# Three microseconds more on every transfer, in the account that orders a three-layer kernel

## The chip, the cores and the metric

The kernel runs on one core of one Trainium2 chip. The metric is the device time of one execution in microseconds (us); the median of several executions is compared. The engines are called PE (matrix products), DVE (vector), ACT (scalar, activations), POOL (general) and SP (which here only issues transfers).

## The reference

The input is a batch of 8 images with 256 channels and 32 x 32 positions. Two layers follow each other:

```python
# layer 0: convolution and attention, on group-normalised x
q  = einsum(x, q_w);  k_map, v_map = einsum(x, kv_w)
ks, vs = layernorm(pooled(k_map)), layernorm(pooled(v_map))   # 4 pooling levels, each + 3x3 depthwise conv: 1426 keys
att = softmax(q @ k * SCALE) @ v                              # 8 heads of 32 channels, 1024 queries
x = x + proj(att @ w_attn)                                    # w_attn: a small matrix per head, from a global token
# layer 1: t = tokens of x, (8, 1024, 256)
t = t + softmax(q @ k * SCALE) @ v                            # one head, of layernorm(t)
t = t + sum_e gate_e * Wo_e(relu(bn(W2_e relu(bn(W1_e layernorm(t))))))   # 8 experts, all of them used
```

The gates are a softmax over the 8 experts of the mean over the batch of the normalised tokens. Everything is float32.

## The kernel before

The kernel has two stages in one program: `attention` (layer 0, and layer 1's attention woven into it) and `experts`.

The backbone of `attention` is a loop over 352 score steps. For each image there are two groups of four heads and two halves of the queries, which makes 32 units; a unit goes through 11 chunks of 128 keys, and a twelfth chunk of 25 keys is handled for four units of an image at once. A step multiplies queries with keys into the score buffer `sc` (four banks of PSUM, one buffer), ACT takes the exponential into a tile `pt` (128 x 2048 floats, 1 MB, six buffers), and one step later PE multiplies `pt` with the values into `pv`. For the sums of the softmax the second `pt` of each two steps is added onto the first by a transfer on POOL's queue (`add`, with `accum_op=ALU.add`): this is the group pt<-pt in the profile. The thread `sums` takes the pairs on from there. In the first four units PE sums each pair directly; from the fifth on DVE adds each pair to the unit's first (two additions of 128 x 1024 for a pair), and PE sums only the result. A pair's buffer is given back (`f.drop`) once that use has been put into the queue.

Everything else is background work, written as Python generators (threads) with a rank: normalising and pooling the next image (`prepare`, which starts with statistics of the freshly loaded image `xi`), convolution taps on DVE (`taps`), keys and values by tokens, the projection of layer 0, and the whole of layer 1 (`layer1`, which loads tokens `t` from memory, and `outputs`). Three more threads read loaded tiles: `weights1` at the start, `experts_ahead` late in the attention stage, and `gates` in the expert stage, which adds seven loaded images `feat` to a sum.

The order of the instructions on each engine is decided while the program is built, by the class `Flow`. It keeps an account: for each engine a clock `now`, for each tile when it is `ready`, who wrote it (`writer`, which is "DMA" for transfers) and when it was last `read`. `note` advances the account with each instruction, by costs from `cost`; `transfer` gives a transfer 2.2 us plus its share of the queues. A thread yields what it needs next: an engine, the tiles that it will read, and possibly a PSUM buffer. Between the pieces of a score step the loop calls `step`, which asks of each thread in order of rank whether it is `runnable`, and lets the first one put its next instructions into the queues. For PE a thread is runnable when its tiles are ready `MARGIN` (1.5 us) ahead of the time at which the score buffer comes free; for another engine, in these lines:

```python
now = self.now[engine]
return now <= pe + AHEAD[engine] if at <= now + 0.3 else at <= pe + NEAR[engine]
```

Here `at` is the latest ready time of the tiles, and `pe` PE's clock. For DVE, AHEAD is 4.0 and NEAR is 1.5. When the program has to wait for something definite (a free `pt`, the next image's keys), it calls `finish`, which picks by `start` in place of `runnable`. On the chip each engine works through its queue in this order and waits at an instruction whose inputs are not there yet.

In `experts` the main loop over tokens and experts is written out by hand; only `gates` and what remains of layer 1 go through `step`. While the gates are not there, units of the first two expert layers are worked ahead and stored. All instructions that go through `Flow` carry line 677 in the profile, so the groups there are told apart by the names of their tiles.

Of the kernel before, what the change touches and what calls it, by code (L numbers as in the profile page):

```python
# [33 lines left out]
CAP = (1.5, 1.5)  # L34
NEVER = 1e9
MARGIN = 1.5
AHEAD = {"DVE": 4.0, "ACT": 2.0, "POOL": 1.0, "SP": 10.0}
NEAR = {"DVE": 1.5, "ACT": 2.0, "POOL": 1.0, "SP": 10.0}
OWN = {"pt", "p1"}
# [624 lines left out]
class Flow:  # L664
# [216 lines left out]
    def spawn(self, gen, rank):  # L881
# [6 lines left out]
            self.threads.insert(at, thread)  # L888
        return thread

    def runnable(self, need, rank=0):
        engine, tiles, tag = need
        if engine is None:
            return tiles()
        at = max([self.ready.get(n, 0.0) for t in tiles for n in self.keys(t)], default=0.0)
        pe = self.now["PE"]
        if engine == "PE":

            until = max(pe, self.free("sc") - 0.5)
            slot = self.free(tag) if tag is not None else 0.0  # L900
            return (
                not self.closed
                and (self.credit[rank >= FILLER] > 0 or pe < until - 0.5)
                and at + MARGIN <= until
                and slot <= until
            )

        now = self.now[engine]
        return now <= pe + AHEAD[engine] if at <= now + 0.3 else at <= pe + NEAR[engine]

# [1981 lines left out]
```

## Time and profile before

| | us |
|---|---|
| median of 3 executions | 3219.64 |
| lowest, highest | 3211.74, 3234.84 |
| the profiled execution, its own time | 3221.01 |
| span of its instructions in the profile | 3219.2 |
| attention stage, up to the last additions of pairs | about 1850 |

The profile is of one execution. It tells each engine's busy time, which instruction it sat idle in front of, and what released it ("<-DMA pt<-pt" is the landing of a pair's transfer). The granted clock of PE was 0.986 of full speed over the span.

### The profile page before, as it was taken

How to read it: one execution, taken by the hardware profiler on the slowest of the kernel's cores; microseconds unless marked ns; L12 is line 12 of the kernel's file. 1: busy time of each engine (PE TensorE's matmuls, PEld its weight loads, DVE VectorE, ACT ScalarE, POOL GpSimd, SP SyncE). 2: the span in 40 equal slices, each digit the busy share in tenths (PEclk: the TensorE clock that was granted, in tenths of full speed). 3: DMA queues.
4: the chain of work that ended last, by engine and by line, in shares of the span. 5: the costliest groups of instructions: out<-in, count | busy, mean ns of one | idle time of the engine just before them, and what ended most of it. 6: DMA issues, size and time to landing. Idle time of an engine off the chain costs nothing.

```text
span 3219.2 us, 55913 instructions
## 1 busy us (share of the span) xinstructions
PE 3063.1 (95%) x22518; PEld 1782.2 (55%) x22518; DVE 2271.2 (71%) x3812; ACT 1624.0 (50%) x2164; POOL 1191.9 (37%) x1321
## 2 busy tenths in 40 slices
PE   7889889989999999989999999999999999999998
PEld 3232224334434433433433357776888888888887
DVE  6865786796887877866544444445887888877776
ACT  3756666567566656666655432334333333334443
POOL 3423242322331422321121120003855555567776
PEclk9899999999999999999999999999999999999999
DMA  1466756666676566566776752214444344320000
GB/s 54 87 150 151 167 117 127 155 131 130 136 169 132 118 150 137 119 152 132 167 164 124 173 212 76 86 72 156 149 146 153 139 161 161 138 78 21 20 14 21
DMA packets 123436, 397.92 MB, mean 124 GB/s; under 512 B 14928, under 2 KB 41080, under 8 KB 99712
## 3 DMA queue, kind: packets, MB, share of 16 engines
q0 software_dynamic: 28608, 181.68, 29.1%
q1 hardware_dynamic: 91056, 210.57, 19.1%
q8 instruction: 180, 2.95, 0.4%
q10 hardware_dynamic: 3504, 1.99, 0.2%
q14 instruction: 88, 0.72, 0.1%
HBM read 129.77 MB, written 97.03 MB: 70 GB/s over the span
## 4 chain that ended last, share of the span: by engine, by line
PE 45%; DVE 3%; issue 1%; POOL 1%; ACT 1%; DMA 1%; DVEq 0%; ACTq 0%; POOLq 0%
PE bank L677 21%; PE y L677 10%; PE sm L677 9%; PE sc L677 2%; PE pv L677 2%; PE sx L677 1%; DVE h L677 1%; DVE u L677 1%; DVE c L677 1%; ACT pt L677 0%; POOL t L677 0%; ACT h L677 0%; DMA pt<-pt 0%; POOL tm L677 0%; DVE t L677 0%
## 5 line engine op out<-in xcount | busy, mean ns | idle before, releaser
L677 ACT ACTIVATE pt<-sc 128x2048 f32<-128x2048 f32 (+1 forms) x352 | 660.6, 1877 | 344.5 <-PE sc L677 290.8
L677 DVE TENSOR_TENSOR pt<-pt,pt 128x1024 f32<-128x1024 f32 x280 | 341.5, 1265 | 237.4 <-DMA pt<-pt 216.0
L677 PE MATMUL sc<-q,kn 32*128 32x512 f32 (+2 forms) x3072 | 423.6, 656 | 72.1 <-ACT pt L677 68.3
L677 PE MATMUL pv<-pt,vt 128*32 128x512 f32 (+1 forms) x2816 | 384.2, 618 | 0.0
L677 POOL TENSOR_TENSOR rstd<-rstd,mhalf 128x4 f32<-128x4 f32 (+2 forms) x88 | 107.3, 1219 | 718.3 <-DVE rstd L677 640.6
L677 ACT ACTIVATE h<-h,bnvec 128x512 f32<-128x512 f32 x432 | 326.6, 805 | 66.5 <-DVE h L677 59.0
L677 ACT ACTIVATE p1c<-bank 128x256 f32<-128x256 f32 x216 | 82.7, 383 | 541.8 <-PE bank L677 524.6
L677 DVE SCALAR_TENSOR_TENSOR acc<-map,vec,acc 128x961 f32<-128x961 f32 (+1 forms) x240 | 310.2, 1295 | 25.8 <-ACT acc L677 20.0
L677 POOL DMA_DIRECT2D pt<-pt x160 | 148.8, 932 | 408.4 <-ACT pt L677 311.8
L677 DVE TENSOR_TENSOR h<-p1c,bank 128x512 f32<-128x512 f32 x216 | 147.3, 682 | 194.6 <-PE bank L677 189.3
L677 PEld LDWEIGHTS sc<-q,kn 32*128 32x128 f32 (+2 forms) x3072 | 114.5, 180 | 251.9 <-ACT pt L677 145.7
L677 DVE TENSOR_TENSOR h<-u,bank 128x256 f32<-128x256 f32 (+1 forms) x432 | 220.0, 550 | 7.4
L677 POOL TENSOR_TENSOR tm<-h,tm 128x256 f32<-128x256 f32 x190 | 218.6, 1151 | 14.9
L677 DVE SCALAR_TENSOR_TENSOR sacc<-small,vec,sacc 128x480 f32<-128x480 f32 (+8 forms) x384 | 201.7, 532 | 13.3 <-ACT sacc L677 3.3
L677 PEld LDWEIGHTS pv<-pt,vt 128*32 128x32 f32 (+1 forms) x2816 | 56.0, 108 | 276.9 <-issue 263.1
L677 PE MATMUL sm<-p,v 128*32 128x256 f32 (+1 forms) x2448 | 201.9, 380 | 4.1 <-DVE turn L677 4.1
L677 DVE TENSOR_TENSOR h<-h,gate 128x1024 f32<-128x1024 f32 x128 | 196.3, 1534 | 0.5 <-ACT h L677 0.5
L677 POOL TENSOR_TENSOR tm<-h 128x512 f32<-128x512 f32 x95 | 123.5, 1300 | 179.6 <-ACT h L677 176.3
L677 PE MATMUL y<-t,s3e 128*128 128x256 f32 x768 | 187.0, 379 | 2.2 <-POOL t L677 2.2
L677 PE MATMUL sm<-y,t 128*32 128x256 f32 (+1 forms) x1896 | 185.1, 379 | 1.2 <-DVE res L677 1.2
L677 PE MATMUL bank<-t,s1e 128*128 128x256 f32 x726 | 176.5, 379 | 0.0
L677 POOL TENSOR_TENSOR t<-h 128x512 f32<-128x512 f32 x98 | 126.7, 1293 | 133.8 <-DVE h L677 90.2
(373 smaller groups left out, 5573.1 us busy)
## 6 DMA issues: line engine op xcount, KB each, us to landing
pt<-pt POOLq DMA_DIRECT2D x160, 1024.0 KB, 7.6
h<-h SPq DMA_DIRECT2D x175, 512.0 KB
xi<-in_x_dram SPq DMA_DIRECT2D x16, 512.0 KB
t<-t SPq DMA_DIRECT2D x8, 1024.0 KB
res<-t SPq DMA_DIRECT2D x32, 256.0 KB
t<-res SPq DMA_DIRECT2D x32, 256.0 KB
hn<-res SPq DMA_DIRECT2D x32, 256.0 KB
hn<-hn SPq DMA_DIRECT2D x16, 512.0 KB
```

The lines of the kernel that those rows point to most:

```text
L677: ins = fn(*args, **kwargs)
```

## The change

A constant `LATE` of 3.0 is added, and `runnable` takes the ready time of each tile through a new method `landed`, which adds `LATE` if the tile's last writer was a transfer.

```diff
 MARGIN = 1.5
+LATE = 3.0
 AHEAD = {"DVE": 4.0, "ACT": 2.0, "POOL": 1.0, "SP": 10.0}
...
+    def landed(self, name):
+
+        return self.ready.get(name, 0.0) + LATE * (self.writer.get(name) == "DMA")
+
     def runnable(self, need, rank=0):
         engine, tiles, tag = need
         if engine is None:
             return tiles()
-        at = max([self.ready.get(n, 0.0) for t in tiles for n in self.keys(t)], default=0.0)
+        at = max([self.landed(n) for t in tiles for n in self.keys(t)], default=0.0)
         pe = self.now["PE"]
```

The account's clocks and ready times themselves, `note`, `start` and `finish` stay as they are. Weights that are loaded outside `Flow`, on ACT's queue at the start, have no writer in the account and are not affected.

## Prediction

> **What bounds the kernel now.** I read the totals first, then the stretches of the span, then what TensorE (PE) and VectorE (DVE) waited for, and last a few single waits in order of time.
>
> ```profile
> span 3219.2 us, 55913 instructions
> PE 3063.1 (95%) x22518; PEld 1782.2 (55%) x22518; DVE 2271.2 (71%) x3812; ACT 1624.0 (50%) x2164; POOL 1191.9 (37%) x1321
> ```
>
> PE is busy for 95% of the span, so all its idle time is 3219.2 - 3063.1 = 156.1 us. [...] I use it only for gaps: an order of instructions takes no matmul away, it can only open or close them. In stretches (columns: busy time of PE, its weight loads, DVE, ACT, POOL, then clock and DMA):
>
> ```profile
> 160.00:480.00 320.00, 279.36 (x2404) 95.53 (x2400) 221.46 (x396) 204.45 (x243) 98.85 (x120) 0.95 0.66 147
> 480.00:800.00 320.00, 304.42 (x3020) 125.44 (x3012) 243.90 (x429) 203.89 (x248) 86.07 (x104) 0.98 0.63 134
> 800.00:1120.00 320.00, 307.14 (x3058) 125.43 (x3062) 259.83 (x472) 200.20 (x240) 98.77 (x123) 0.99 0.65 141
> 1120.00:1440.00 320.00, 300.38 (x3056) 120.95 (x3052) 243.21 (x420) 195.72 (x231) 83.05 (x103) 0.99 0.64 140
> 1440.00:1760.00 320.00, 313.70 (x3448) 120.36 (x3440) 178.76 (x335) 192.84 (x207) 62.03 (x70) 0.99 0.69 146
> ...
> 1920.00:2240.00 320.00, 320.00 (x1282) 235.26 (x1281) 151.34 (x309) 114.95 (x191) 33.01 (x46) 1.00 0.28 99
> ```
>
> The attention stage ends near 1850. PE's gaps in the first five rows are 40.6, 15.6, 12.9, 19.6 and 6.3, together 95.0 us. From 1920 to 2240 there is none. So whatever the order account changes has to show up in those 95 us (3% of the span).
>
> Then the waits that a late transfer causes, DVE first, PE below:
>
> ```profile
> DVE pt L677 <- DMA pt<-pt: 216.0, 67, 12.1
> ...
> PE sc L677 <- ACT pt L677: 68.3, 71, 3.4
> PE sx L677 <- DMA pt<-pt: 10.1, 2, 8.5
> PE sm L677 <- DVE st L677: 5.2, 1, 5.2
> PE sm L677 <- DMA t<-t: 1.0, 1, 1.0
> ```
>
> DVE stood 216.0 us in 67 waits (3.2 us each) in front of an addition whose second operand, a pair of exponentials summed by a POOL transfer, had not landed. PE's own largest wait is another one: the next scores wait for ACT to read the one score buffer out. One piece of DVE's time shows that the 216 us are not all lost:
>
> ```profile
> 1212.70 0.16 DVE L677 SCALAR_TENSOR_TENSOR tshift<-tmean,rstd 128x4 f32<-128x4 f32 x1
> 1224.91 2.75 DVE L677 TENSOR_TENSOR pt<-pt,pt 128x1024 f32<-128x1024 f32 x2 [12.06 <-DMA pt<-pt]
> ...
> 1223.42 0.77 ACT L677 ACTIVATE acc<-sm,vec,mid 128x512 f32<-128x512 f32 x1
> ```
>
> This is the longest of the 67. Behind the additions stand convolution taps on an accumulator that ACT finished at 1224.19, so with the addition placed later DVE would have gained 0.7 of these 12.06 us. In the second longest (9.43 us, ending at 772.94) the accumulator was done at 771.05: 1.9 us. Long waits are mostly an empty queue, not a blocked one.
>
> Two places do reach PE:
>
> ```profile
> 209.74 1.94 PE L677 MATMUL sx<-pt,con 128*32 128x512 f32 x8 [8.52 <-DMA pt<-pt]
> ...
> 390.01 1.29 DVE L677 BATCH_NORM_STATS2 st<-xi 128x6 f32<-128x512 f32 x2 [5.16 <-DMA xi<-in_x_dram]
> ...
> 395.94 0.59 PE L677 MATMUL sm<-mv,con 128*128 128x2 f32 x2 [5.23 <-DVE st L677]
> ```
>
> [...] 7.6 us median to landing, 3.8 to 15.5. [...]
>
> **The change part by part.** It removes and adds no instruction, no transfer and no semaphore. It changes when a waiting thread counts as ready: if one of its tiles was last written by a transfer, three microseconds of the account's time are added. Only the test `runnable` sees them; `start`, used when the program must drain, does not, nor does the account's own clock. For a pair the account has 1.0 for the issue and 2.2 + 1048.6 KB x 0.0036 = 5.97 for the transfer, 6.97 in all, 0.6 under the trace's median; with the three it is 9.97, which covers all but the slow tail.
>
> Affected are: 140 pair additions on DVE (280 instructions), the PE sums of the first four units (24 tests), two statistics reads of the image per batch, the eight loads of layer 1's tokens, seven gate additions, and single weight loads. Not affected: everything in the expert loop after the gates, which is written out by hand, so the 980 us after 2240 keep their order except for which units were staged.
>
> *Direct waits of PE.* Placed three later, 8.5 becomes 5.5, the other PE wait for pairs (1.6) goes, 1.0 goes, 5.2 becomes 2.2: 3.0 + 1.6 + 1.0 + 3.0 = 8.6 us gained, if other PE work stands ready. Bounds: 0 (no filler) to 15.3 (waits 8.5 + 1.6 + 5.2 all gone).
>
> *DVE.* The ceiling is 67 waits x 3 us = 201 us. The two waits above gave back 2.6 of 21.5, so I take between a tenth and a half of 201, 20 to 100 us of DVE. PE gains only where it waits for DVE: from 160 to 1850 that is 4.1 (turn), 3.8 (res), 2.1 (t), 1.6 (s) and 0.9 (xl), 12.5 us without the 5.2 counted. I take a third, 4 us; bounds 0 to 12.5, and more only if earlier taps give PE fillers that it lacks (rival one).
>
> *Buffers held longer.* A pair is dropped after its second addition is queued, so it is held up to 3 us longer; there are six buffers, and a step of scores comes about every 1760/352 = 5 us. So 0.6 of the 140 pairs, 84, are held over one more step. Today ACT waits 17.5 us (8 times) for a pair's transfer before writing a buffer and about 6.5 us (3 times) for DVE, 2.2 us each. Behind that exponential on ACT stand copies of projections and convolution maps, and PE's next scores wait for it. I let one in ten of the 84 wait: 8 x 2.2 = 18 us on ACT, half of it covered by fillers on PE: 9 us lost. Bounds: 0 to 46 (half of the 84 waiting).
>
> *Layer 1's loads* are used three later eight times; 0 to 24 us, covered by other fillers; I take 2. *The gates* come after 1887.9, their last load is issued at 2174.3, and PE has no gap there to widen: 0; uncovered it would be 3. *The drain at the end of attention* goes by `start`: 0. POOL's and SP's queues get no instruction moved past them on purpose; their issues follow the threads by the same few us.
>
> Sum: -8.6 - 4 + 9 + 2 = -1.6 us against the profiled execution's 3221.01 (span 3219.2 and 1.8 around it), 3219.4. That execution stands 1.4 over the median 3219.64, so the forecast in terms of the median is 3218.
>
> **Rivals.** *One: DVE was the pacemaker.* If half of the 201 us comes back as earlier taps, the next batch's key and value work is there sooner and fills PE. For: DVE is busy 76 to 81% from 480 to 1440 and waiting much of the rest. Against: its longest waits had nothing behind them, and PE's waits for it are small. Price: 40% of the 95 us of gaps, 38: 3182.
>
> *Two, slower: the six buffers run short.* Mechanism as above, in the attention stage at the start of each exponential: half of the 84 held pairs make ACT wait 2.2 us, half of that is bare on PE: 46, less 4 that DVE still gives: 3262. It decides once ACT's waits for buffers pass some 60 us (24 today). For: those waits exist already and feed PE's largest wait. Against: 341 of 352 steps find a buffer free today.
>
> *Three: nothing reaches PE.* The account orders the same work slightly otherwise and every gap stays within a few us: 3220.
>
> **How the numbers follow.** Forecast 0.45, rival three 0.08, rival one 0.22, rival two 0.25. The forecast's own range is 3192 (both gains at their bounds, 15.3 and 12.5, nothing lost) to 3240 (nothing gained, the 18 us of ACT bare on PE, and 2). An order of thousands of instructions can move either way by more than its parts, so the range for 8 in 10 reaches to both rivals' values: 3182 to 3262. Over 1% (32 us) is about what a measurement of this kernel can tell from no change; the forecast and rival three lie within it (0.53), rival one beyond below (0.22), rival two beyond above (0.25).
>
> **What would show it.** Right: DVE's wait for pairs falls from 216 to below 170 but not to 50; PE's wait of 8.5 and of 5.2 shrink to 3 to 6; ACT's waits for buffers grow to 30 to 50; PE's gaps from 160 to 1760 stay at 80 to 110 us; 1920 to 2240 stays full. Rival one: PE's gaps fall below 65. Rival two: ACT's waits for buffers pass 60 and PE's wait of the scores for ACT passes 100. The forecast is wrong in kind if PE's busy time itself moves by over 15 us, or if the end of attention (1850) moves by over 30.

## The result, and the profile after

| | before | after |
|---|---|---|
| median, us | 3220.52 | 3178.8 (3174.91 to 3181.38) |
| ratio | | 0.9875, interval 0.985 to 0.9899 |
| span of the profiled execution, us | 3219.2 | 3176.1 |

The median of before is that of its runs beside after. The changed kernel is 1.25% faster, 42 us by these medians. The forecast was no change (3218), with 3182 as the lower end of its range. All `Flow` instructions now carry line 678.

The totals of after, at the head of its profile page:

```profile
span 3176.1 us, 56426 instructions
PE 3052.5 (96%) x22778; PEld 1794.2 (56%) x22778; DVE 2284.5 (72%) x3823; ACT 1627.8 (51%) x2175; POOL 1287.8 (41%) x1387
```

The span is 43.1 us shorter. PE's idle time went from 156.1 to 3176.1 - 3052.5 = 123.6 us, 32.5 less; its busy time fell by 10.6 us although the same result is computed. The instructions are not quite the same ones (56426 in the profile, in place of 55913), since the order also decides how products are cut up and where the function `warm` puts fillers. These are products of a constant tile with itself, issued where the account sees PE idle for 1.8 us or more. In the trace they are 40 matmuls (2.5 us) in before, 108 (9.2 us) in after. The stretches of after, with the columns as in the prediction:

```profile
160.00:480.00 320.00, 290.05 (x2670) 103.89 (x2666) 226.35 (x399) 210.50 (x256) 105.47 (x122) 0.98 0.67 147
480.00:800.00 320.00, 307.96 (x3127) 125.78 (x3120) 240.55 (x434) 202.84 (x245) 88.66 (x104) 0.99 0.65 139
800.00:1120.00 320.00, 308.61 (x3280) 124.29 (x3280) 268.21 (x494) 196.72 (x231) 97.82 (x120) 0.99 0.66 143
1120.00:1440.00 320.00, 307.91 (x3018) 123.65 (x3020) 252.88 (x425) 216.09 (x269) 100.44 (x115) 1.00 0.65 140
1440.00:1760.00 320.00, 315.05 (x3452) 126.46 (x3448) 172.75 (x329) 185.76 (x189) 61.30 (x68) 1.00 0.70 149
1920.00:2240.00 320.00, 317.02 (x1293) 240.84 (x1292) 192.71 (x309) 114.97 (x189) 120.42 (x156) 0.99 0.42 145
```

The gaps of the first five rows are 30.0, 12.0, 11.4, 12.1 and 5.0, 70.4 in all against 95.0. Each stretch gave some, but in 5.1 of the 24.6 us PE only runs more fillers. The clock column rose in four of the five rows, by 0.03 in the first and 0.01 in the others. This can be where busy time went: in before a product pv<-pt,vt of 128x512 took 614 ns in the median outside the stretches at half rate (see the last section), and 1061 ns inside them. The last row is new: it is no longer quite full (3.0 us of gaps).

The waits of after (us in total, times, longest):

```profile
DVE pt L678 <- DMA pt<-pt: 111.1, 34, 13.6
...
PE sc L678 <- ACT pt L678: 48.2, 63, 3.0
...
PE sm L678 <- DVE mv L678: 15.8, 2, 10.3
...
ACT pt L678 <- DMA pt<-pt: 12.2, 7, 3.3
...
PE sx L678 <- DMA pt<-pt: 3.5, 1, 3.5
```

DVE's wait for pairs halved, from 216.0 to 111.1. Yet all of DVE's waits from 160 to 1850 together fell only from 465 to 450: those for PE went from 109 to 178 and those for ACT from 79 to 107. What fell for PE is mostly not a wait for DVE or for a transfer: the scores' wait for ACT lost 20.1 us, the direct wait for a pair 6.6. PE's waits for DVE, all together, did not fall: from 160 to 1850 they are 17.9 us in before and 23.1 in after, while those for ACT went from 66.3 to 46.3. So the halved wait of DVE is not itself the gain.

The attention stage's last addition of a pair starts at 1830 in place of 1847, 17 us earlier. The other 26 us come later, where less of layer 1 is left to do, since more of it was done inside the attention stage. The transfers that write its tokens out (count: shortest, median and longest time of the issuing instruction in ns; then the first and the last issue in us), before and after:

```profile
L677 SPq DMA_DIRECT2D hn<-res x32: 512/528/1377, 574.0 to 2171.2; - x32
```
```profile
L678 SPq DMA_DIRECT2D hn<-res x32: 512/527/1638, 537.9 to 2063.3; - x32
```

Layer 1's last tokens leave 108 us earlier, so the gates come earlier and fewer expert units must be stored and fetched again. The page counts these transfers:

```profile
h<-h SPq DMA_DIRECT2D x175, 512.0 KB
```
```profile
h<-h SPq DMA_DIRECT2D x111, 512.0 KB
```

That is 64 transfers, a store and a fetch for 32 units.

### The profile page after: what moved, and what is told of

Read it like the earlier page. It is cut to its first block, busy times and chain, and to the rows that moved or that the text cites. A ratio compares the mean times of both kernels' runs of the same rounds, so it can differ in the third digit from the quotient of the medians.

```text
span 3176.1 us, 56426 instructions
## 1 busy us (share of the span) xinstructions
PE 3052.5 (96%) x22778; PEld 1794.2 (56%) x22778; DVE 2284.5 (72%) x3823; ACT 1627.8 (51%) x2175; POOL 1287.8 (41%) x1387
## 4 chain that ended last, share of the span: by engine, by line
PE 70%; DVE 8%; issue 3%; ACT 3%; DMA 3%; POOL 2%; SPq 0%; DVEq 0%; POOLq 0%; ACTq 0%
PE bank L678 21%; PE sm L678 16%; PE y L678 10%; PE sc L678 8%; PE sx L678 7%; PE pv L678 7%; DVE acc L678 2%; ACT pt L678 2%; DMA pt<-pt 2%; DVE pt L678 1%; DVE h L678 1%; DVE u L678 1%; DVE c L678 1%; DMA xi<-in_x_dram 1%; ACT h L678 0%
## 5 line engine op out<-in xcount | busy, mean ns | idle before, releaser
L678 PE MATMUL sc<-q,kn 32*128 32x512 f32 (+2 forms) x3072 | 417.9, 649 | 49.4 <-ACT pt L678 48.2
L678 DVE TENSOR_TENSOR pt<-pt,pt 128x1024 f32<-128x1024 f32 x280 | 340.6, 1261 | 113.9 <-DMA pt<-pt 111.1
L678 ACT ACTIVATE h<-h,bnvec 128x512 f32<-128x512 f32 x454 | 343.4, 805 | 65.8 <-DVE h L678 55.6
L678 DVE TENSOR_TENSOR h<-p1c,bank 128x512 f32<-128x512 f32 x227 | 154.7, 682 | 201.6 <-PE bank L678 198.5
L678 POOL TENSOR_TENSOR tm<-h,tm 128x256 f32<-128x256 f32 x212 | 242.8, 1145 | 16.6
L678 DVE TENSOR_TENSOR h<-u,bank 128x256 f32<-128x256 f32 x454 | 231.3, 550 | 7.8
L678 POOL TENSOR_TENSOR tm<-h 128x512 f32<-128x512 f32 x106 | 140.1, 1321 | 200.1 <-ACT h L678 198.0
L678 DVE SCALAR_TENSOR_TENSOR sacc<-small,vec,sacc 128x480 f32<-128x480 f32 (+8 forms) x384 | 194.8, 515 | 14.9 <-ACT sacc L678 4.7
L678 POOL TENSOR_TENSOR t<-h,t 128x256 f32<-128x256 f32 x218 | 173.8, 797 | 17.1
L678 POOL TENSOR_TENSOR t<-h 128x512 f32<-128x512 f32 x109 | 141.4, 1297 | 94.8 <-DVE h L678 74.1
L678 DVE TENSOR_TENSOR u<-h,bank 128x512 f32<-128x512 f32 x227 | 156.1, 688 | 25.1 <-PE bank L678 0.8
```

The source lines that it names most:

```text
L678: ins = fn(*args, **kwargs)
```

## The experiments

Three ideas run through the expectations. First, DVE's wait is itself the cost: take it away and DVE's time comes back. Second, chance: any small change gives another order of 56,000 instructions, and orders differ. Third, formed after the first results (theory C where a letter is used): DVE time that the account did not plan. If the account believed that a pair lands at the moment at which DVE reaches its addition, and it lands later, all that stands behind it on DVE, and then on ACT and PE, comes later than the order was made for. Time that DVE idles because the account planned it would cost nothing of the kind.

For the third idea each instruction's start in the account is set beside its start on the chip. Two numbers follow. The *unplanned wait* is the sum, over the first addition of each pair, of DVE's idle time in the trace beyond what the account had there. The *lag* is a DVE instruction's start in the trace less its start in the account. With the account's own end of PE's work (us; the lag near the times at the head):

```
              median  DVE wait  unplanned  account's  lag at
                      for pairs   wait      PE end    330   800  1300  1800
before        3220.5   216.0      94.2      3146.8    20.2  42.2  48.2  46.5
after         3178.8   111.1      47.3      3137.9    14.3  22.5  23.2  16.8
pairs_only    3169.4   117.2      49.3      3153.2    12.5   4.0   3.6  -6.8
all_but_pairs 3222.9   265.1     124.9      3142.3                      55.3
margin_1_4    3226.2   225.9     110.7      3147.2                      59.9
half_adds     3194.9   265.9     105.9      3120.0                      47.7
pairs_dve     3194.7   143.4      57.1      3146.6                      21.2
pairs_6       3193.6    63.0      33.0      3151.7                       7.2
pairs_m2      3285.1   289.7     148.0      3175.2                      75.5
next_pair     3231.9   129.4      76.3      3156.2                      39.3
unplanned     3257.0   177.7      76.9+97   3146.8    22.0  53.5  73.6  79.6
planned       3225.6   175.8      82.2      3150.8                      60.6
account_pool  3196.4   168.1      45.6      3170.1                      -3.7
pairs_4       3182.2    91.7      37.5      3151.9                       1.7
all_but_image 3196.3   122.2      58.1      3154.4                      19.9
pairs_pe      3221.6   254.7     112.5      3159.7                      34.6
pairs_margin  3185.5   112.1      42.9      3151.5                       7.6
```

The median is nearly the account's end plus the lag at 1800 plus a constant: over these 17 kernels the constant is 27 us with a standard deviation of 5.5. This is close to a matter of definition: it tells which of two terms a change moved, and not why. Before's lag grows to 48 and stays; pairs_only's goes back to nothing.

### Which tiles carry the gain

**pairs_only**: three microseconds for the pairs alone.

```diff
-        return self.ready.get(name, 0.0) + LATE * (self.writer.get(name) == "DMA")
+        return self.ready.get(name, 0.0) + LATE * (self.writer.get(name) == "DMA" and name.startswith("pt"))
```

> LATE of 3 us for the pairs of exponentials alone (tiles pt last written by a transfer), not for any other loaded tile. If DVE standing in front of pairs was what cost (rival one): nearly the whole gain, 3180 to 3190, DVE's wait for pairs near 110 us, PE's gaps from 160 to 1760 near 75 us. If the gain came from the image statistics, layer 1's loads or the gates: 3210 to 3225, with DVE's wait for pairs still falling to about 110. If any change of order gives a scatter of 30 to 40 us: anything from 3180 to 3250, with no relation to DVE's wait.

Measured: 3169.38, ratio 0.9845 (0.9828 to 0.9861). The pairs carry all of it. Its row for the attention stage, to set beside before's 1504.99 us of busy PE in the same window:

```profile
160.00:1760.00 1600.00, 1533.77 (x15480) 612.15 (x15474) 1166.84 (x2084) 1014.78 (x1189) 438.70 (x528) 1.00 0.67 145
```

PE's gaps are 1600 - 1533.77 = 66.2 us against 95.0; 14 of these 29 us are fillers (16.8 us against 2.5). The account of this order ends 6 us later than before's; the lag fell by 53. The gain is in the lag alone.

**all_but_pairs**: the same line with `and not name.startswith("pt")`.

> LATE of 3 us for every loaded tile except the pairs of exponentials. If the pairs carry the gain: 3210 to 3225, DVE's wait for pairs stays near 216 us; a few us may come from the PE wait of 5.2 behind the image statistics. If the other loads carry it: 3180 to 3190. If order scatter: anything from 3180 to 3250.

Measured: 3222.93, ratio 1.0015 (1.0003 to 1.0027). The image, layer 1's tokens, the gates' loads and the single weights bring nothing together.

**all_but_image**: with `and not name.startswith("xi")`, so that of all loads only the image is left out.

> The changed kernel, but without LATE for the freshly loaded image xi (LATE for pairs, tokens, gates and weights stays). In the changed kernel PE waits 15.8 us for the image's statistics (two waits, the longer 10.3), with pairs alone 9.1. If placing those statistics later is what costs the 10 us between pairs alone and the whole change: 3167 to 3174. If it is scatter of the order: 3174 to 3190.

Measured: 3196.29, ratio 0.9938 (0.9918 to 0.9958). This is 17.5 us over after. Both ranges expected lie below it. Either the image is worth that much beside the pairs, which pairs_only (9 us under after, with no image) speaks against, or it is the scatter between orders.

**pairs_dve** and **pairs_pe**: the pairs alone, and only where DVE, or only where PE, is to read them. For DVE:

```diff
-        at = max([self.landed(n) for t in tiles for n in self.keys(t)], default=0.0)
+        at = max([self.landed(n) if engine == "DVE" and n.startswith("pt") else self.ready.get(n, 0.0) for t in tiles for n in self.keys(t)], default=0.0)
```

> LATE of 3 us for the pairs in front of DVE additions only; the PE sums of the first four units are placed as before. Theory A (DVE, stopped in front of a pair, holds back everything behind it, and PE and ACT get it late): 3170 to 3182, DVE's wait for pairs near 115 us, PE's wait of 8.5 us for a pair back. Theory B (the first four units' PE sums carry a good part, because the whole account drifts from the chip there): 3190 to 3205.

> LATE of 3 us only for pairs in front of PE's sums, in the first four units; DVE's additions are placed as before. The wait of 8.5 us on PE and the half-rate clock after it should shrink: 3200 to 3212 by what that stretch holds (some 10 to 15 us). If the 25 us between DVE alone (3195) and all pairs (3169) belong wholly to these sums: 3190 to 3200. If they are scatter: 3212 to 3225.

Measured: pairs_dve 3194.65, ratio 0.9918 (0.9899 to 0.9937); pairs_pe 3221.64, ratio 1.0005 (0.9996 to 1.0015). For PE alone, the direct wait does shrink, and DVE's stays. The waits of pairs_pe:

```profile
DVE pt L678 <- DMA pt<-pt: 254.7, 71, 15.0
...
PE sx L678 <- DMA pt<-pt: 3.5, 1, 3.5
```

PE's wait of 10.1 became 3.5, just as in after, and the time did not move. So lateness where DVE reads the pairs gains 26 us by itself (by the ratio), and where PE reads them nothing. But both together, in pairs_only, gain 50. pairs_dve lies in the range of theory B, by which PE's sums carry the other 24, and pairs_pe lies where scatter was expected. Whether the 24 us need both or are a lucky order stays open.

### Chance

**margin_1_4**: before, with `MARGIN = 1.4` in place of 1.5. **pairs_margin**: the same in pairs_only.

> The kernel before with MARGIN 1.4 in place of 1.5: no LATE, only a slightly different order, DVE's wait for pairs expected near 216 us. If order scatter is small: within 10 us of before, 3210 to 3230. If scatter of the order is as large as the measured 42 us, it lands 20 us or more away from before, on either side, and the gain of the change can't be put down to the DVE waits without more evidence.

> Pairs alone with 3 us, and MARGIN 1.4 in place of 1.5 beside it: a measure of how far a neighbouring order lies. If pairs alone at 3169 is a lucky order within the mechanism: 3180 to 3200. If scatter is as small as with MARGIN 1.4 on the kernel before (+6): 3163 to 3178.

Measured: margin_1_4 3226.19, ratio 1.0019 (1.0009 to 1.0028); pairs_margin 3185.46, ratio 0.9903 (0.9877 to 0.993), 16 us over pairs_only. So an order that is merely another one differs by 6 to 16 us. The four orders with no lateness on DVE's pairs (before, all_but_pairs, margin_1_4, pairs_pe) lie between 3220 and 3226; the five with three microseconds there (after, pairs_only, pairs_dve, all_but_image, pairs_margin) between 3169 and 3196. With pairs_4 and pairs_6 below, also under 3196, the second group has seven. The two groups are 24 us apart and do not overlap, so chance alone is a very unlikely cause of the gain; within the second group, differences of up to 27 us are not explained and may be chance. Nor do the fillers explain it: pairs_pe has 208 of them (14.1 us) and gains nothing, after only 108.

### How much lateness

**pairs_m2**, **pairs_4**, **pairs_6**: pairs_only with `LATE` at -2.0, 4.0 and 6.0.

> Pairs alone, 2 us EARLIER than the account has them (LATE -2). Theory A: DVE's wait for pairs grows to 280 to 350 us and the time goes up by 15 to 40 us, to 3235 to 3260. If the gain was one lucky order among many (order scatter): about as likely below 3220 as above.

> Pairs alone, 4 us. Between the measured 3 us (3169) and 6 us (3194): 3165 to 3190, DVE's wait for pairs 80 to 110 us, ACT's waits for a buffer between 32 and 60 us. It tells whether the best value lies above 3.

> Pairs alone, 6 us in place of 3. Theory A: DVE's wait for pairs falls further, below 90 us, and the time stays within 10 us of 3169, unless the buffers run short. Rival (six buffers run short, as the prediction's second rival had it): ACT's waits for a buffer (on pair transfers and on DVE's additions) pass 60 us and the time goes back above 3185.

Measured: 3285.12, ratio 1.0202 (1.0176 to 1.0228); 3182.21, ratio 0.9888 (0.986 to 0.9915); 3193.61, ratio 0.9912 (0.9893 to 0.9931). Two microseconds earlier costs 65 us, more than the 15 to 40 that theory A allowed, with more waiting of DVE for pairs and of PE's scores for ACT. The waits of pairs_m2:

```profile
DVE pt L678 <- DMA pt<-pt: 289.7, 83, 14.3
...
PE sc L678 <- ACT pt L678: 89.6, 88, 4.1
```

From three upward the time does not fall any more although DVE's wait still does; at six it misses theory A's range and comes to that of its rival, short buffers. At six, ACT's waits for a free pair buffer show a price. The waits of pairs_6:

```profile
DVE pt L678 <- DMA pt<-pt: 63.0, 15, 10.2
...
ACT pt L678 <- DMA pt<-pt: 33.0, 9, 6.6
...
ACT pt L678 <- DVE pt L678: 27.0, 8, 5.3
```

The same two of before:

```profile
ACT pt L677 <- DMA pt<-pt: 17.5, 8, 3.5
...
ACT pt L677 <- DVE pt L677: 7.9, 5, 2.5
```

33.0 + 27.0 = 60 us on ACT, against 25.4 in before. Whether this alone makes six worse than three cannot be told apart from the scatter of 16 us.

### Is it DVE's wait?

**half_adds** leaves out the second of each pair's two additions (half of a pair's columns are not summed): 140 instructions of DVE less (median 1219 ns each in before).

```diff
-                for j in range(0, 4, 2):
+                for j in range(0, 2, 2):
```

> The kernel before, with the second of the two DVE additions of each pair left out (heads 2 and 3 of a group are summed over the first pair only), in the account too. DVE loses 140 x 1.22 = 171 us of busy time in the attention stage. If DVE time paces the fillers of PE (rival one): faster than the changed kernel, 3150 to 3180, PE's gaps from 160 to 1760 below 75 us. If DVE time is worth little there: 3205 to 3225.

Measured: 3194.9, ratio 0.9925 (0.9908 to 0.9942), with DVE's wait for pairs at 265.9 us, more than before's. Its stretch of the attention stage, and then that of before:

```profile
160.00:1760.00 1600.00, 1519.92 (x15884) 593.26 (x15880) 1017.50 (x1955) 999.24 (x1175) 422.86 (x524) 0.99 0.66 143
```
```profile
160.00:1760.00 1600.00, 1504.99 (x14962) 587.70 (x14954) 1147.17 (x2048) 997.10 (x1166) 428.77 (x520) 0.98 0.65 141
```

DVE is busy 130 us less, and the kernel gains 24 by the ratio, between the two ranges expected. All of that is in the account's end (3146.8 to 3120.0); the lag is the same (46.5 to 47.7). So work taken from DVE and lateness given to its pairs gain in different terms, and DVE's load has a price.

**next_pair**: before's account, but a pair is added only once the next pair's transfer has been issued.

```diff
-                yield until(lambda: len(pairs) > i)
+                yield until(lambda: len(pairs) > min(i + 1, NKC // 2 - 1))
```

> The kernel before without LATE, but each pair is added only once the next pair's transfer has been issued (the last one of a unit as before), some 11 us later, so nearly every landing is long past; one more buffer is held. Theory A: DVE's wait for pairs below 60 us (the last pair of each unit stays) and 3165 to 3190. If buffers run short: ACT's waits for a buffer pass 60 us and 3200 to 3240. Order scatter: no relation to DVE's wait.

Measured: 3231.9, ratio 1.0026 (1.0005 to 1.0047). DVE's wait for pairs fell by 87 us, nearly as much as in after:

```profile
DVE pt L677 <- DMA pt<-pt: 129.4, 33, 10.9
```

and nothing was gained. The account shows the difference: of the waits that went, most were planned ones. The account's own idle time in front of first additions fell from 194.3 to 125.5 us, the unplanned wait only from 94.2 to 76.3, and the account's end got 9 us worse, perhaps because additions now come in bursts. The size of DVE's wait alone does not set the time: half_adds waits more and gains, next_pair waits less and does not.

### Is it the unplanned time?

**unplanned** and **planned** add the same instruction 140 times, a product by 1.0 on the sum tile after the first addition of each pair. In the first it is issued past the account, in the second through it.

```diff
                     f.ve.tensor_tensor(s, s, pairs[i][: rows[i], j : j + 2, :], ALU.add)
+                    if j == 0:
+                        nc.vector.tensor_scalar(s, s, 1.0, None, ALU.mult)   # planned: f.ve.tensor_scalar
```

> The kernel before plus 140 multiplications of 128 x 1024 by one on DVE, one for each added pair, that the account does not know of (about 0.9 us each, some 120 us of DVE). Theory C (what costs is DVE time that the account did not plan, since everything behind it then runs later than the order was made for): 40 to 90 us slower than before, 3260 to 3310, and the lag of the trace behind the account's clock at the end of attention grows from 46 us to 90 or more. The prediction's view (DVE has slack, its lateness hardly reaches PE): within 15 us of before.

> The same 140 multiplications, but issued through the account, so that they are planned. Theory C: clearly less than the unplanned ones cost, 5 to 35 us over before (3225 to 3255), with the lag at the end of attention near 46 us as before. If DVE time as such is what paces PE (rival one as the prediction had it): the same cost as the unplanned ones, within 15 us.

In before a TENSOR_SCALAR of 128x1024 on DVE (xi<-xi,mu,gr) took 890 ns in the mean. The added instruction in the trace, first of unplanned, then of planned (shortest, median and longest in ns, first and last start in us):

```profile
L1735 DVE TENSOR_SCALAR pt<-pt x140: 679/686/1615, 341.7 to 1882.2; 128x1024 f32<-128x1024 f32 x112, 121x1024 f32<-121x1024 f32 x28
```
```profile
L677 DVE TENSOR_SCALAR pt<-pt x140: 693/694/1607, 346.0 to 1837.7; 128x1024 f32<-128x1024 f32 x112, 121x1024 f32<-121x1024 f32 x28
```

Measured: unplanned 3256.95, ratio 1.012 (1.0092 to 1.0148), just under the range of theory C (its lag too, which was to reach 90); planned 3225.57, ratio 1.0018 (1.0005 to 1.003). The same work of about 140 x 0.69 = 97 us on DVE costs 39 us (by the ratio) where the account does not know it and 6 where it does. unplanned has before's order instruction by instruction, and its lag grows from 22.0 at 330 to 79.6 at 1800, 33 over before's. What it issues differs from before in these 140 instructions alone. This shows that DVE time outside the account costs by itself, and about how much: 33/97 of it in the lag, 39/97 in the time.

Two things do not fit so well. The lag of planned was to stay near 46 us and is 60.6, with less unplanned wait than in before, so the lag has other sources too. And the sizes do not close. At 33/97, an estimate from these two runs, the 47 us of unplanned wait that after saves would give 16 of the 30 us of its lag, and 45 us in pairs_only 15 of 53. Counted in the traces, what DVE waited at additions beyond the account, less what it waited there under it, put 40 us on the lag between 330 and 1800 in before, 22 in after and 19 in pairs_only. The growth of the lag over that stretch fell by 24 and by 46 us. So additions account for 17 of the 24 and 21 of the 46; the rest is in DVE's other waits.

**account_pool**: the three microseconds go into the account's clocks themselves, for every transfer on POOL's queue, in place of the test.

```diff
-        return 2.2 + left[mine] + min(left[mine], left[other]) + self.served - at
+        return 2.2 + 3.0 * (queue == "POOL") + left[mine] + min(left[mine], left[other]) + self.served - at
```

> The kernel before without LATE; instead the account itself lets every transfer of POOL's queue land 3 us later, in its clocks as well as in the order. Theory C: the lag of the trace behind the account at the end of attention falls from 46 to below 25 us, DVE's unplanned waits halve, and the time is 3165 to 3195, as with LATE. If it is only the placement test that matters and the planned clocks cost something: 3195 to 3220.

Measured: 3196.37, ratio 0.9935 (0.9912 to 0.9958). The lag is gone (-3.7), in part by definition, since the account's own times moved to later ones; the account's end is 23 us worse. The time lies at the border of the two ranges expected. The change as made, which delays consumers and leaves the clocks alone, lowers the lag by 30 us and has no such loss: its account ends 9 us earlier than before's.

## Why the prediction was wrong

**What bounds the kernel** held in the main: PE's gaps gave 32.5 of the 43.1 us of the span. But the prediction took PE's busy time as fixed, and it fell by 10.6 us (see the last section). Nor is it so that the change adds and removes no instruction: the fillers and the transfers of expert units above differ.

**Direct waits of PE (-8.6 us)**: the one of 8.5 became 3.5, about as said. That of 5.2 for the image did not shrink:

```profile
398.21 0.58 PE L678 MATMUL sm<-mv,con 128*128 128x2 f32 x2 [5.52 <-DVE mv L678]
```

No gain is seen from this: pairs_pe removed 6.6 us of such waits with a ratio of 1.0005, though a few us could hide in the scatter between orders.

**DVE (-4 us)**: this is the step that failed. It had two parts. "Long waits are mostly an empty queue" was right, and the account says how right: of the 237 us of idle in front of first additions in before, 143 lie within what the account had planned there. The other 94 got no price beyond what PE lost in direct waits for DVE, "a third" of 12.5 us. Those direct waits were the wrong place to look: PE's waits for DVE rose by 5 us while the kernel gained 42. What the runs show in its place is that lateness on DVE is not paid where it arises. It adds up to a lag of 46.5 us at 1800, which after cuts by 29.7. With the account's end 8.9 better, this makes 38.6 of the 41.7 us.

The longest wait, whose line the prediction shows, is an example. Of its 12.06 us up to 1224.91 the account had planned 8.8. DVE was 44.2 us behind the account before it and 47.4 after it, and the taps that follow were 47.6 behind. The prediction had asked only whether a tap was ready during the wait (0.7 us), and not what the 3 us did to all that came later.

By which way a late DVE reaches PE is not shown. PE's waits for ACT fell, and ACT itself waits for DVE's additions (7.9 us in before); the largest of PE's, the scores' wait, which the prediction called "another one", went from 68.3 to 48.2 us. But in pairs_4 and pairs_6 it is 67.3 and 69.1, and they gain 36 and 28 us by the ratio.

**Buffers held longer (+9 us)**: not borne out. ACT's waits for buffers (17.5 + 7.9 in before; the prediction read the second as 6.5) went down to 12.2 in after. Other orders with three microseconds have more, 32.5 in pairs_only and 50.0 in pairs_dve, and gain all the same. They reach the 60 us at which rival two was to decide only at six, and there the kernel is still 0.9% faster than before.

**Layer 1's loads (+2 us), the gates and the drain (0)**: all_but_pairs, which has these and the image, is at 1.0015. What no step had is that layer 1 ends 108 us earlier and fewer expert units are stored.

**The rivals**: rival one gave 3182 and its sign, PE's gaps below 65, was nearly met (70.4). It had the right engine: the gain comes through DVE. Its mechanism was not met: DVE did not get half of 201 us back, its waits fell by 15 in all. And PE's gaps from 160 to 1760 fell by 25 in place of 38, the rest coming from PE's busy time and from later gaps. That its number lies so near is in part luck. Rival three, that nothing reaches PE, falls. Of the two signs that the forecast would be wrong in kind, neither came: PE's busy time moved by 10.6 and the end of attention by 17. One of the signs that it would be right did come, DVE's wait between 50 and 170 (111.1), and it says little: next_pair has 129.4 and gains nothing. Others did not: ACT's waits for buffers fell in place of growing to 30 to 50, PE's gaps left the range of 80 to 110, and 1920 to 2240 did not stay full.

What stays open is the spread of 27 us among the orders with three microseconds, and why the account's end differs by up to 16.5 us between them.

**pairs_only is the best version**: 3169.38, under both before and after. Its distance to after (9 us) is within what another order alone gives.

## What to carry to other kernels

Where queues are in order and an account decides the order, ask of an idle stretch whether the account knew of it. Here DVE stood in front of a pair for the last 0.7 us up to 1224.91 in before, with the input of the taps behind it ready. In this kernel planned idle time of DVE could go without a gain (the account's own fell by 69 us in next_pair, at a ratio of 1.0026), while unplanned time of DVE moved what stood behind it and added up (97 us in unplanned put 33 on the lag). Whether this holds for other engines was not tried. Reading the account's start of each instruction beside the trace's start separates a bad plan (the account's end) from a plan not kept (the lag). If a landing time scatters, as a pair's did (in before a median of 7.6 us from issue to landing, 15.5 at most), try to place its consumers by the late side of it and leave the clocks at the median; of the values tried here three microseconds did best, though not clearly beyond the scatter. Watch whether the buffers that are held longer begin to make others wait (60 us on ACT in pairs_6). An order that is merely another one moved this kernel by 6 to 16 us, so a single run of a changed order proves little below that.

## What the runs showed of the hardware

In before and after PE's granted clock fell to one half in stretches of 3.4, 6.8 or 10.2 us (one at the end of the program apart, 9.3 us in before and 7.3 in after). In the attention stage there are 16 in before and 10 in after, and each begins during a gap of PE or within 2 us after one. (One at 2085.5 in after has no gap ahead of it.) The wait of 8.52 us that ended at 209.74 in before is an example; its window of 20 us, and the same window of after, where PE has no such gap:

```profile
200.00:220.00 20.00, 11.48 (x73) 3.19 (x70) 15.02 (x34) 6.89 (x6) 1.28 (x3) 0.74 0.79 183
```
```profile
200.00:220.00 20.00, 20.00 (x164) 7.91 (x164) 16.73 (x44) 11.25 (x15) 3.22 (x5) 0.97 0.76 164
```

In before the mean clock is 0.74, since 10.2 us from 204.8 on are at one half: this begins inside the gap, and PE does what follows it at half rate until 215.0. All such stretches add up to 94.6 us in before (mean clock 0.986), 58.5 in after (0.991), 50.3 in pairs_only (0.992), 110.7 in unplanned and 111.0 in pairs_m2 (both 0.983). The gap of 8.52 us thus cost more than its length, and closing such gaps can lower busy time too. An estimate from these sums and the clock: 36 us fewer at half rate save at most half of that, 18 us of busy time; busy time fell by 10.6, with 6.7 us of fillers more in it. The sum does not set the time, though: pairs_pe has 61.7 us at half rate (mean clock 0.991) and is no faster than before.

The length of a gap alone does not tell whether such a stretch follows. In before gaps of 1.62 us (from 1189.3 on), 2.54 (1101.8) and 1.68 (646.3) were followed by 3.4 us at half rate, the largest gaps ahead of those stretches; after gaps of 2.16 us (699.2) and 2.25 us (903.9) none began. What sets the onset and the length of a stretch was not shown.
